# A small network beside a streaming statistics pass: fewer array passes, one transfer queue, deeper buffers

## The chip, the cores and the metric

The kernel runs on one core of one Trainium2 chip. The core has a matrix engine (TensorE, "PE" in the profile, with its weight loads as "PEld"), a vector engine (VectorE, "DVE"), a scalar engine (ScalarE, "ACT"), a general engine (GpSimd, "POOL") and a synchronising engine (SyncE, "SP"). SP and ACT can each put transfers on a queue of their own; the engine that issues a transfer stands still while it waits for its turn ("SPq", "ACTq" in the profile). The metric is the device time of one execution in microseconds (us), as the median of several. All data are fp32.

## The reference, cut to what matters

Two layers are computed one after the other. Each normalizes its input over groups of channels, applies a convolution whose weights differ at every position and batch (they come out of a small network), and adds the result to its input.

```python
S2, B, CI, CO, L, K, A, H = (32, 32, 64, 64, 256, 3, 16, 128)
def _ln(h, g, b):                      # mean and variance over the 128 hidden units
    ...
h  = relu(_ln(z @ W1 + b1, g1, be1))   # z: (B, L, 16); first small network
w  = (h @ W2 + b2).reshape(B, L, CI, CO, K)
hb = relu(_ln(z @ Wb1 + bb1, gb1, beb1))           # second small network
bias = (hb @ Wb2 + bb2).transpose(0, 2, 1)
out = einsum('sbilk,bliok->sbol', windows_of(x), w) + bias[None]
# x = x + conv(groupnorm(x)), for layer 0 and then for layer 1
```

The statistics of the first normalization run over all of the input x, 32 x 32 x 64 x 256 fp32 numbers, so nothing of the convolution of layer 0 can be finished before x has been read once.

## The kernel before

The kernel has two parts. A **first phase** streams x through on-chip memory in 16 transfers of 4 MB, and VectorE takes statistics of it (256 `bn_stats` instructions). Beside that, in the same stretch of time, the small networks of both layers are evaluated for all batches, in 32 steps of two batches each: a step makes the hidden units `hd` and the bias `bd`, which go to HBM and are read back later. The **main part** then runs the convolutions of both layers. The change touches only the first phase.

A step is split over three turns of the pipeline. In turn `s` the kernel projects step `s`, scales step `s-1` and makes the bias of step `s-2`:

```python
class Hidden:
    def __init__(self, stage, zts, small, i):
        self.zt = zts[i % NZ]                       # NZ = 4, one z tile for a step
        ...
        self.sq = flat[:, i % 3 * w : ...]          # 3 buffers
        self.ht = flat[:, (3 + i % 4) * w : ...]    # 4 buffers, both networks
        self.bs = flat[:, 7 * w + i % 4 * L : ...]  # 4 buffers

    def project(self):                              # PE, then ACT
        self.p1 = ps_g.tile([P, NBLK, 2, P], ...)   # NBLK = 4
        for k in range(NBLK):
            for r in range(0, P, C):                # C = 64: two groups of array columns
                a = k * P + r
                nc.tensor.matmul(self.p1[r : r + C, k], self.zt[:, a : a + C], self.t["wc"], ...)
        nc.scalar.activation(self.sq, self.p1..., AF.Square)

    def sums(self):        # POOL: 7 additions that halve the width, to the variance
    def root(self):        # ACT: square root
    def scale(self):
        nc.vector.reciprocal(self.var, self.var)
        nc.vector.tensor_tensor(...)                # first half of the rows
        for k in range(n, 2 * NBLK):
            nc.scalar.activation(hs[:, k], p1[:, k], AF.Copy, scale=...)   # second half
        for k in range(NBLK):
            for net in range(2):
                nc.tensor.transpose(p2[:, net, k * P : (k + 1) * P], hs[:, 2 * k + net, :], ident)
        for net in range(2):
            nc.scalar.activation(self.ht[:, net, :], p2[:, net, :], AF.Relu, ...)
        nc.scalar.dma_start(out=hd[self.i]..., in_=self.ht[:, 0, :]...)
    def bias(self):
        for b in range(2):
            nc.tensor.matmul(p3[b * C : (b + 1) * C], self.t["Wb2"], self.ht[:, 1, ...], ...)
        nc.scalar.activation(self.bs, p3..., AF.Identity, bias=...)
        for b in range(2):
            nc.scalar.dma_start(out=bd[self.i][b]..., in_=self.bs[...]...)
```

The steps are laid between the statistics instructions, three of those to each half turn:

```python
def step(s, half):
    if half == 0:
        if s - 1 in made: made[s - 1].root()
        if s < U // 2:                              # U // 2 = 32
            made[s] = Hidden(stage, zts, small, s)
            made[s].project(); made[s].sums()
            load_z(s + NZ, nc.scalar)
    else:
        if s - 1 in made: made[s - 1].scale()
        if s - 2 in made: made.pop(s - 2).bias()

SQ = SV // NH * GT                                  # 16 statistics for one 4 MB load
first, last = 4, (NQ - 3) * SQ                      # NQ = 16, so last = 208
n = U + 4                                           # 68 half turns
when = {first + k * (last - first) // n: k for k in range(n)}
for i in range(NQ * SQ):                            # 256
    if i in (2, first + n):
        center(stage, small[k], k)                  # take the mean off the small weights
    if i in when:
        step(*divmod(when[i], 2))
    if i == (NQ - 2) * SQ:
        first_weights()                             # first weights of the main part, PE and ACT
    bn_stats(...)
    if i % SQ < SQ - 1: continue
    if q + 3 < NQ: load(q + 3)                      # on SP, into the place just read
    ...                                             # W2 in four parts, hidden units, on SP
```

Three places hold loads of x, so a load goes out when the statistics three loads earlier are done. In the program as it is built, the transfers of both queues take eight completion semaphores in turn, in the order of the program: before a transfer is issued, its engine waits until the transfer eight places earlier has landed, whichever queue that was on.

Of the kernel before, what the change touches and what calls it, by code (L numbers as in the profile page):

```python
# [23 lines left out]
FP = mybir.dt.float32  # L24
AF = mybir.ActivationFunctionType
ALU = mybir.AluOpType
# [4 lines left out]
P = 128  # L31
# [10 lines left out]
def conv_layers(ctx: ExitStack, tc: tile.TileContext, xs: bass.AP, xp: bass.AP, layers: list, out: bass.AP):  # L42


    nc = tc.nc
    B, _, M, S = xp.shape
    SH, C, L = S // 2, P // 2, 2 * M
    A = layers[0]["z"].shape[0]
# [10 lines left out]
    U = NL * B  # L59
    SV = 4  # L60
    BLK = 2 * L
    NBLK = BLK // P
    NZ = 4
    RING = 3
    assert 2 * C == P and NT * S == P and M == P and BLK == 512 and EB == 2 * E

# [50 lines left out]
    def load_b2(n):  # L117
        nc.sync.dma_start(out=b2[n], in_=layers[n]["b2"])
# [20 lines left out]

    def load_small(stage, par, n):  # L140

        t = {}
        for name in ("wc", "vec", "Wb2"):
            shape = list(par[name].shape)
            t[name] = stage.tile(shape, FP, name=f"{name}_{n}")
            nc.sync.dma_start(out=t[name], in_=par[name])
        return t

    def center(stage, t, n):

        wc = t["wc"]
        m = stage.tile([A + 1, 2], FP, name=f"wm_{n}")
        nc.vector.tensor_reduce(m, wc, AX.X, ALU.add)
        nc.vector.tensor_scalar(m, m, -1.0 / P, None, ALU.mult)
        nc.vector.tensor_tensor(wc, wc, m[:, :, None].to_broadcast([A + 1, 2, P]), ALU.add)  # L155

    class Hidden:


        def __init__(self, stage, zts, small, i):  # L160
            self.stage, self.i, self.t = stage, i, small[i // (B // 2)]
            self.zt = zts[i % NZ]

            flat = xn.rearrange("p b m s -> p (b m s)")
            w = 2 * NBLK * P
            self.sq = flat[:, i % 3 * w : (i % 3 + 1) * w].rearrange("p (n h) -> p n h", h=P)
            self.ht = flat[:, (3 + i % 4) * w : (4 + i % 4) * w].rearrange("p (n f) -> p n f", f=BLK)
            self.bs = flat[:, 7 * w + i % 4 * L : 7 * w + (i % 4 + 1) * L]
            self.bs = self.bs.rearrange("p (t a m) -> p t a m", t=NT, a=2)

        def project(self):
            self.p1 = ps_g.tile([P, NBLK, 2, P], FP, tag="pg", name="p1")
            for k in range(NBLK):
                for r in range(0, P, C):
                    a = k * P + r
                    nc.tensor.matmul(  # L176
                        self.p1[r : r + C, k], self.zt[:, a : a + C], self.t["wc"], start=True, stop=True
                    )
            nc.scalar.activation(self.sq, self.p1.rearrange("p k n h -> p (k n) h"), AF.Square)  # L179

        def sums(self):
# [10 lines left out]
        def scale(self):  # L192
            nc.vector.reciprocal(self.var, self.var)  # L193
            hs, p1 = self.sq, self.p1.rearrange("p k n h -> p (k n) h")
            n = NBLK
            nc.vector.tensor_tensor(  # L196
                hs[:, 0:n], p1[:, 0:n], self.var[:, 0:n, None].to_broadcast([P, n, P]), ALU.mult
            )
            for k in range(n, 2 * NBLK):
                nc.scalar.activation(hs[:, k], p1[:, k], AF.Copy, scale=self.var[:, k : k + 1])  # L200
            p2 = ps_g.tile([P, 2, BLK], FP, tag="pg", name="p2")
            for k in range(NBLK):
                for net in range(2):
                    nc.tensor.transpose(p2[:, net, k * P : (k + 1) * P], hs[:, 2 * k + net, :], ident)  # L204
            for net in range(2):
                nc.scalar.activation(  # L206
                    self.ht[:, net, :],
                    p2[:, net, :],
                    AF.Relu,
                    bias=self.t["vec"][:, 2 * net + 1 : 2 * net + 2],  # L210
                    scale=self.t["vec"][:, 2 * net : 2 * net + 1],
                )
            nc.scalar.dma_start(
                out=hd[self.i].rearrange("b p f -> p b f"),
                in_=self.ht[:, 0, :].rearrange("p (b f) -> p b f", b=2),
            )

        def bias(self):
            p3 = ps_c.tile([P, L], FP, tag="pc", name="p3")
            for b in range(2):  # L220
                nc.tensor.matmul(  # L221
                    p3[b * C : (b + 1) * C],
                    self.t["Wb2"],
                    self.ht[:, 1, b * L : (b + 1) * L],
                    start=True,
                    stop=True,
                )
            nc.scalar.activation(
                self.bs,
                p3.rearrange("p (a t m) -> p t a m", a=2, t=NT),  # L230
                AF.Identity,
                bias=self.t["vec"][:, 4:5],
            )
            for b in range(2):
                nc.scalar.dma_start(  # L235
                    out=bd[self.i][b].rearrange("t o l -> o t l"),
                    in_=self.bs[b * C : (b + 1) * C].rearrange("p t a m -> p t (a m)"),
                )
# [3 lines left out]
    def bn_stats(out, y, g):  # L242
        e = E // 2
        nc.vector.bn_stats(out, y.rearrange("p o (a m) -> p o a m", a=2)[:, :, :, g * e : (g + 1) * e])  # L244

    def first_phase(first_weights):


        NQ = NH * B // SV
        w = SV * CH * LT  # L250
# [7 lines left out]
        def load(q, step=SV):  # L258
            for j in range(0, SV, step):
                nc.sync.dma_start(  # L260
                    out=xv[q][:, j : j + step], in_=xs[:, q * SV + j : q * SV + j + step]
                )

        def work(stage):
            zts = []
            for j in range(NZ):
                zts.append(stage.tile([A + 1, BLK], FP, name=f"zt_{j}"))
                nc.gpsimd.memset(zts[j], 1.0)

            def load_z(i, eng):  # L270
                if i < U // 2:
                    n, j = divmod(i, B // 2)
                    eng.dma_start(out=zts[i % NZ][0:A], in_=layers[n]["z"][:, j * BLK : (j + 1) * BLK])

            small = [load_small(stage, layers[0], 0)]
            load_z(0, nc.sync)
            load(0, 1)
            for j in range(1, NZ):
                load_z(j, nc.sync)
            load(1)  # L280
            small.append(load_small(stage, layers[1], 1))
            load(2)
            for n in range(NL):
                load_b2(n)
            made = {}

            def step(s, half):

                if half == 0:
                    if s - 1 in made:  # L290
                        made[s - 1].root()
                    if s < U // 2:
                        made[s] = Hidden(stage, zts, small, s)
                        made[s].project()
                        made[s].sums()
                        load_z(s + NZ, nc.scalar)
                else:
                    if s - 1 in made:
                        made[s - 1].scale()
                    if s - 2 in made:  # L300
                        made.pop(s - 2).bias()

            SQ = SV // NH * GT
            first, last = 4, (NQ - 3) * SQ
            n = U + 4
            when = {first + k * (last - first) // n: k for k in range(n)}
            for i in range(NQ * SQ):
                if i in (2, first + n):
                    k = int(i > 2)
                    center(stage, small[k], k)  # L310
                if i in when:
                    step(*divmod(when[i], 2))
                if i == (NQ - 2) * SQ:
                    first_weights()
                u, g = divmod(i, GT)
                q, j = divmod(u, SV // NH)
                bn_stats(first_parts[:, g, u, 0, :], xu[q][:, j], g)
                if i % SQ < SQ - 1:
                    continue
                if q + 3 < NQ:  # L320
                    load(q + 3)
# [392 lines left out]
```

## Time and profile before

| what | value |
|---|---|
| time, median of 3 runs | 4096.45 us (4092.12 to 4099.84) |
| span of the profiled execution | 4089.9 us |
| PE busy over the span | 3927.3 us (96%) |
| last statistics instruction of the first phase ends | 309.5 us |
| first product of the main part starts | 342.6 us |
| moved from the start to 320 us | 93.10 MB, 291 GB/s on average |

The page divides the span into 40 slices, and one slice is about 102 us. The first phase therefore fills three slices, and its own limits have to be read from windows of the trace, not from the totals. "PEclk" is the clock granted to the matrix engine, as a share of full speed. "Issue" in a chain of waits is time in which an engine waited for nothing that the profile shows, and "ACTq L235" is ScalarE busy with handing a transfer of line 235 to its queue.

### The profile page before, as it was taken

What the parts mean: (1) busy time and instruction counts of PE and PEld (TensorE: products, weight loads), DVE (VectorE), ACT (ScalarE), POOL (GpSimd) and SP (SyncE); (2) the same over time, 40 slices, a digit from 0 to 9 for tenths busy, and PEclk for the clock granted to TensorE, in tenths of its full rate; (3) what the DMA queues carried; (4) which work ended last, traced back from release to release, by engine and by line L of the source; (5) the groups of instructions that cost most, each with busy time, mean ns of one, the idle gap of its engine ahead of it and who ended that gap; (6) DMA issues with size and microseconds to landing.
All of it is one profiled execution on the core that took longest, in us unless ns stands there. A gap on an engine that the chain in (4) does not pass through costs nothing.

```text
span 4089.9 us, 194766 instructions
## 1 busy us (share of the span) xinstructions
PE 3927.3 (96%) x91064; PEld 3737.5 (91%) x91064; DVE 2602.2 (64%) x2934; ACT 1337.8 (33%) x4480; POOL 1946.6 (48%) x638
## 2 busy tenths in 40 slices
PE   6888999999999999999998999999999999999999
PEld 3447999999999999999998999999999999999999
DVE  4566666666666676666666565656555565656565
ACT  4553323233333333232323332323333333323332
POOL 3435435534553454345443655545554455445541
PEclk6558999999999999999999999999999999999999
DMA  8876777777777777777777544444444454445442
GB/s 305 309 284 160 195 174 195 175 191 179 184 187 183 187 182 186 173 194 172 190 171 190 178 150 146 153 143 155 154 145 158 140 166 133 160 139 169 137 148 89
DMA packets 654877, 718.55 MB, mean 176 GB/s; under 512 B 567378, under 2 KB 584052, under 8 KB 585588
## 3 DMA queue, kind: packets, MB, share of 16 engines
q1 hardware_dynamic: 627060, 692.59, 59.9%
q8 instruction: 711, 11.65, 1.2%
q10 hardware_dynamic: 27008, 13.51, 1.1%
q14 instruction: 98, 0.80, 0.1%
HBM read 492.08 MB, written 213.91 MB: 173 GB/s over the span
## 4 chain that ended last, share of the span: by engine, by line
PE 88%; DVE 6%; DMA 2%; issue 2%; ACT 1%; POOL 1%; ACTq 1%; SPq 0%; DVEq 0%; POOLq 0%
PE pg L482 50%; PE pc L528 23%; PE pg L483 12%; DVE wall L494 2%; DVE parts L244 2%; PE p L176 2%; PE p L204 1%; DMA room<-in_xs_dram 1%; DVE room L538 1%; POOL xn L469 1%; ACTq L235 0%; DMA bd<-xn 0%; PE p L221 0%; DMA hd<-xn 0%; ACT xn L179 0%
## 5 line engine op out<-in xcount | busy, mean ns | idle before, releaser
L482 PE MATMUL pg<-hT,w2t 128*64 128x128 f32 x24576 | 2737.1, 273 | 28.2 <-DVE wall L494 11.2
L483 PE MATMUL pg<-hT,w2t 128*64 128x128 f32 x24576 | 2736.5, 273 | 4.3 <-issue 3.9
L482 PEld LDWEIGHTS pg<-hT,w2t 128*64 128x64 f32 x24576 | 2681.5, 137 | 55.9 <-DVE wall L494 23.6
L483 PEld LDWEIGHTS pg<-hT,w2t 128*64 128x64 f32 x24576 | 2682.2, 137 | 7.8 <-issue 6.8
L494 DVE TENSOR_TENSOR wall<-pg,b 64x1024 f32<-64x1024 f32 x1527 | 1855.6, 1220 | 688.9 <-PE pg L483 685.2
L505 ACT ACTIVATE wall<-pg,b 64x128 f32<-64x128 f32 x4168 | 1191.7, 479 | 2585.2 <-DVE wall L494 2157.6
L451 POOL TENSOR_TENSOR xn<-room,gmean 128x2048 f32<-128x2048 f32 x124 | 572.7, 4619 | 1758.1 <-PE pc L528 1728.2
L528 PEld LDWEIGHTS pc<-wall,xn 128*32 128x32 f32 x40960 | 932.2, 111 | 99.4 <-issue 83.9
L528 PE MATMUL pc<-wall,xn 128*32 128x128 f32 (+2 forms) x40960 | 974.2, 253 | 50.8 <-issue 37.8
L538 DVE TENSOR_TENSOR room<-pc,room 128x512 f32<-128x512 f32 x512 | 354.2, 692 | 656.2 <-PE pc L528 583.6
L451 POOL TENSOR_TENSOR xn<-xn,rstd 128x2048 f32<-128x2048 f32 x124 | 656.5, 5294 | 9.7
L418 POOL TENSOR_TENSOR room<-room,bt 128x2048 f32<-128x2048 f32 x128 | 588.5, 4597 | 120.2 <-DMA bt<-bd 49.6
L244 DVE BATCH_NORM_STATS2 parts<-room 128x6 f32<-128x256 f32 (+1 forms) x592 | 241.5, 453 | 8.7
L187 POOL TENSOR_TENSOR xn<-xn 128x512 f32<-128x512 f32 (+2 forms) x192 | 104.1, 542 | 156.3 <-ACT xn L179 143.8
L176 PE MATMUL p<-wc,zt 17*64 17x256 f32 x512 | 116.1, 628 | 12.3 <-DVE wc L155 12.3
L204 PEld LDWEIGHTS p<-ident,xn 128*128 128x128 f32 x256 | 47.4, 207 | 87.9 <-issue 66.1
L176 PEld LDWEIGHTS p<-wc,zt 17*64 17x64 f32 x512 | 53.7, 217 | 71.8 <-issue 71.0
L204 PE MATMUL p<-ident,xn 128*128 128x128 f32 x256 | 69.6, 438 | 50.2 <-DVE xn L196 35.9
L244 DVE BATCH_NORM_STATS2 parts<-wall 128x6 f32<-128x512 f32 x160 | 97.7, 677 | 11.2 <-DMA wall<-in_xs_dram 11.2
L193 DVE RECIPROCAL var<-var 128x8 f32<-128x8 f32 x32 | 6.5, 203 | 111.0 <-ACT var L190 111.0
L206 ACT ACTIVATE xn<-p,vec 128x512 f32<-128x512 f32 x64 | 46.3, 773 | 22.1 <-PE p L204 22.1
L179 ACT ACTIVATE xn<-p 128x1024 f32<-128x1024 f32 x32 | 32.6, 1019 | 36.0 <-PE p L176 35.7
(58 smaller groups left out, 239.5 us busy)
## 6 DMA issues: line engine op xcount, KB each, us to landing
bt<-bd SPq DMA_DIRECT2D x512, 256.0 KB, 6.5
room<-in_xp_dram SPq DMA_DIRECT2D x64, 1024.0 KB, 9.4
room<-in_xs_dram SPq DMA_DIRECT2D x64, 1024.0 KB, 8.6
x<-room SPq DMA_DIRECT2D x64, 1024.0 KB, 5.3
x1p<-room SPq DMA_DIRECT2D x512, 128.0 KB, 6.8
room<-x1p SPq DMA_DIRECT2D x64, 1024.0 KB, 8.0
room<-x SPq DMA_DIRECT2D x64, 1024.0 KB, 8.3
out_dram<-room SPq DMA_DIRECT2D x64, 1024.0 KB, 4.9
```

The source lines that it names most:

```text
L176: nc.tensor.matmul(self.p1[r : r + C, k], self.zt[:, a : a + C], self.t["wc"], start=True, stop=True)
L187: nc.gpsimd.tensor_tensor(to, self.sq[:, :, 0:w], self.sq[:, :, w : 2 * w], ALU.add)
L204: nc.tensor.transpose(p2[:, net, k * P : (k + 1) * P], hs[:, 2 * k + net, :], ident)
L244: nc.vector.bn_stats(out, y.rearrange("p o (a m) -> p o a m", a=2)[:, :, :, g * e : (g + 1) * e])
L418: nc.gpsimd.tensor_tensor(y, y, bts.pop(v), ALU.add)
L451: nc.gpsimd.tensor_tensor(o, i, b.to_broadcast(list(o.shape)), op)
L482: nc.tensor.matmul(pg[0:C, k, :], w[:, k0 * C : (k0 + 1) * C], h0, start=True, stop=True)
L483: nc.tensor.matmul(pg[C:P, k, :], w[:, k1 * C : (k1 + 1) * C], h1, start=True, stop=True)
L494: nc.vector.tensor_tensor(place(rows, a), pg[rows].rearrange("p o (t m) -> p t m o", t=NT), b2[n][rows, kind, None, None, o0 : o0 + OG].to ...
L505: nc.scalar.activation(place(rows, a)[:, :, :, k], pg[rows, k].rearrange("p (t m) -> p t m", t=NT), AF.Identity, bias=b2[n][rows, kind, o0 ...
L528: nc.tensor.matmul(pc[t * S : (t + 1) * S, n0 - q * EB : n1 - q * EB, :], xn[:, u % 2, t * MT + p + 1, :], wall[:, t, a : a + (n1 - n0) * CH],
L538: nc.vector.tensor_tensor(part, pc.rearrange("p (m a) o -> p o a m", a=2), part, ALU.add)
```

## The change

The change rebuilds how the small networks are fed and drained in the first phase. It does five things.

1. **Projections in two groups of array rows.** The contraction has 17 rows (16 inputs and a row of ones for the bias). The z tile and the weights are laid out twice, at partitions 0 and 32, so that half of the blocks go through array rows 0 to 31 and the other half through rows 32 to 63. With the two groups of columns that were there, four products can be in the array at a time.
2. **All transfers by SP's queue.** The stores of hidden units and biases, and the loads of z, move from ScalarE's queue to SP's.
3. **Buffers.** Hidden units that are stored get 6 buffers and those that are only read by the bias product get 2 (4 for both before); biases get 8 (4 before); squares get 2 (3 before). The z tiles hold two steps each, and there are 3 of them.
4. **Weights centred first.** The centring goes ahead of the first statistics instruction (`i == 0` in place of 2), and the steps begin at `i == 1` in place of 4.
5. The end of the steps (`last`) stays, and so does everything after the first phase. The spreading of the statistics, by 4 matmuls in the first layer and by 24 in the second, is the same in both kernels.

```diff
-    NZ = 4
+    NZ = 3
+    ZB = 2
+    R = 32
...
+        t = {"wc": stage.tile([R + A + 1, 2, P], FP, name=f"wc_{n}")}
+        nc.gpsimd.memset(t["wc"], 0.0)
+        for r in (0, R):
+            nc.sync.dma_start(out=t["wc"][r : r + A + 1], in_=par["wc"])
...
-            self.zt = zts[i % NZ]
+            self.zt = zts[i // ZB % NZ][:, i % ZB * 2 * P : (i % ZB + 1) * 2 * P]
...
-            self.sq = flat[:, i % 3 * w : (i % 3 + 1) * w]...
-            self.ht = flat[:, (3 + i % 4) * w : (4 + i % 4) * w]...
-            self.bs = flat[:, 7 * w + i % 4 * L : 7 * w + (i % 4 + 1) * L]
+            self.sq = flat[:, i % 2 * w : (i % 2 + 1) * w]...
+            self.ht = [flat[:, (4 + j) * BLK : (5 + j) * BLK] for j in (i % 6, 6 + i % 2)]
+            self.bs = flat[:, 6 * w + i % 8 * L : 6 * w + (i % 8 + 1) * L]
...
-            for k in range(NBLK):
+            for k in range(NBLK // 2):
                 for r in range(0, P, C):
-                    a = k * P + r
-                    nc.tensor.matmul(
-                        self.p1[r : r + C, k], self.zt[:, a : a + C], self.t["wc"], start=True, stop=True
-                    )
+                    for j in range(2):
+                        rows = slice(j * R, j * R + A + 1)
+                        nc.tensor.matmul(
+                            self.p1[r : r + C, 2 * j + k],
+                            self.zt[rows, k * P + r : k * P + r + C],
+                            self.t["wc"][rows],
+                            start=True,
+                            stop=True,
+                        )
...
-            nc.scalar.dma_start(                     # hd; the two stores of bd likewise
+            nc.sync.dma_start(
...
-            def load_z(i, eng):                      # one transfer for a step
+            def load_z(b):                           # two transfers, on SP, for two steps
...
-                        load_z(s + NZ, nc.scalar)
+                        if s % ZB == ZB - 1:
+                            load_z(s // ZB + NZ)
...
-            first, last = 4, (NQ - 3) * SQ
+            first, last = 1, (NQ - 3) * SQ
...
-                if i in (2, first + n):
+                if i in (0, first + n):
```

More of the change, by code (lines that the diff above doesn't have):

```diff
@@ L140, in load_small @@
     def load_small(stage, par, n):
-        t = {}
-        for name in ("wc", "vec", "Wb2"):
+        t = {"wc": stage.tile([R + A + 1, 2, P], FP, name=f"wc_{n}")}
+        nc.gpsimd.memset(t["wc"], 0.0)
+        for r in (0, R):
+            nc.sync.dma_start(
+                out=t["wc"][r : r + A + 1], in_=par["wc"]
+            )
+        for name in ("vec", "Wb2"):
             shape = list(par[name].shape)
@@ L151, in center @@
         wc = t["wc"]
-        m = stage.tile([A + 1, 2], FP, name=f"wm_{n}")
+        m = stage.tile([R + A + 1, 2], FP, name=f"wm_{n}")
         nc.vector.tensor_reduce(m, wc, AX.X, ALU.add)
         nc.vector.tensor_scalar(m, m, -1.0 / P, None, ALU.mult)
-        nc.vector.tensor_tensor(wc, wc, m[:, :, None].to_broadcast([A + 1, 2, P]), ALU.add)
+        nc.vector.tensor_tensor(wc, wc, m[:, :, None].to_broadcast([R + A + 1, 2, P]), ALU.add)
     class Hidden:
@@ L161, in __init__ @@
             self.stage, self.i, self.t = stage, i, small[i // (B // 2)]
-            self.zt = zts[i % NZ]
+            self.zt = zts[i // ZB % NZ][:, i % ZB * 2 * P : (i % ZB + 1) * 2 * P]
             flat = xn.rearrange("p b m s -> p (b m s)")
             w = 2 * NBLK * P
-            self.sq = flat[:, i % 3 * w : (i % 3 + 1) * w].rearrange("p (n h) -> p n h", h=P)
-            self.ht = flat[:, (3 + i % 4) * w : (4 + i % 4) * w].rearrange("p (n f) -> p n f", f=BLK)
-            self.bs = flat[:, 7 * w + i % 4 * L : 7 * w + (i % 4 + 1) * L]
+            self.sq = flat[:, i % 2 * w : (i % 2 + 1) * w].rearrange("p (n h) -> p n h", h=P)
+            self.ht = [flat[:, (4 + j) * BLK : (5 + j) * BLK] for j in (i % 6, 6 + i % 2)]
+            self.bs = flat[:, 6 * w + i % 8 * L : 6 * w + (i % 8 + 1) * L]
             self.bs = self.bs.rearrange("p (t a m) -> p t a m", t=NT, a=2)
@@ L172, in project @@
             self.p1 = ps_g.tile([P, NBLK, 2, P], FP, tag="pg", name="p1")
-            for k in range(NBLK):
+            for k in range(NBLK // 2):
                 for r in range(0, P, C):
-                    a = k * P + r
-                    nc.tensor.matmul(
-                        self.p1[r : r + C, k], self.zt[:, a : a + C], self.t["wc"], start=True, stop=True
-                    )
+                    for j in range(2):
[6 more added lines that the diff above has]
+                            stop=True,
+                        )
             nc.scalar.activation(self.sq, self.p1.rearrange("p k n h -> p (k n) h"), AF.Square)
@@ L206, in scale @@
                 nc.scalar.activation(
-                    self.ht[:, net, :],
+                    self.ht[net],
                     p2[:, net, :],
@@ L212, in scale @@
                 )
-            nc.scalar.dma_start(
+            nc.sync.dma_start(
                 out=hd[self.i].rearrange("b p f -> p b f"),
-                in_=self.ht[:, 0, :].rearrange("p (b f) -> p b f", b=2),
+                in_=self.ht[0].rearrange("p (b f) -> p b f", b=2),
             )
@@ L223, in bias @@
                     self.t["Wb2"],
-                    self.ht[:, 1, b * L : (b + 1) * L],
+                    self.ht[1][:, b * L : (b + 1) * L],
                     start=True,
@@ L234, in bias @@
             for b in range(2):
-                nc.scalar.dma_start(
+                nc.sync.dma_start(
                     out=bd[self.i][b].rearrange("t o l -> o t l"),
@@ L266, in work @@
             for j in range(NZ):
-                zts.append(stage.tile([A + 1, BLK], FP, name=f"zt_{j}"))
+                zts.append(stage.tile([R + A + 1, ZB * BLK // 2], FP, name=f"zt_{j}"))
                 nc.gpsimd.memset(zts[j], 1.0)
-            def load_z(i, eng):
-                if i < U // 2:
-                    n, j = divmod(i, B // 2)
-                    eng.dma_start(out=zts[i % NZ][0:A], in_=layers[n]["z"][:, j * BLK : (j + 1) * BLK])
+            def load_z(b):
+                if b * ZB < U // 2:
+                    n, i = divmod(b * ZB, B // 2)
+                    z = layers[n]["z"][:, i * BLK : (i + ZB) * BLK].rearrange("a (k j f) -> a k j f", k=ZB, j=2)
+                    for j in range(2):
+                        nc.sync.dma_start(
+                            out=zts[b % NZ][j * R : j * R + A].rearrange("a (k f) -> a k f", k=ZB),
+                            in_=z[:, :, j],
+                        )
             small = [load_small(stage, layers[0], 0)]
-            load_z(0, nc.sync)
+            load_z(0)
             load(0, 1)
             for j in range(1, NZ):
-                load_z(j, nc.sync)
+                load_z(j)
             load(1)
@@ L307, in work @@
             for i in range(NQ * SQ):
-                if i in (2, first + n):
-                    k = int(i > 2)
+                if i in (0, first + n):
+                    k = int(i > 0)
                     center(stage, small[k], k)
```

## The prediction

> **What bounds the kernel now.** I read the page first, then the busy time by stretches, then the chain of waits through the middle of the first phase, then who waited for whom, and last the queues.
>
> ```profile
> PE 3927.3 (96%) x91064; PEld 3737.5 (91%) x91064; DVE 2602.2 (64%) x2934; ACT 1337.8 (33%) x4480; POOL 1946.6 (48%) x638
> ...
> PEclk6558999999999999999999999999999999999999
> ```
>
> ```profile
> core 0: us, PE busy (x) PEld busy (x) DVE busy (x) ACT busy (x) POOL busy (x), PEclk, DMA share, GB/s
> 0.00:21.70 21.70, 7.32 (x32) 3.77 (x32) 9.07 (x19) 4.19 (x5) 5.98 (x17) 1.00 0.90 341
> 21.70:275.70 254.00, 205.97 (x848) 104.68 (x848) 140.09 (x253) 129.22 (x278) 107.18 (x217) 0.53 0.82 295
> 275.70:309.50 33.80, 23.73 (x304) 21.01 (x304) 33.78 (x57) 26.39 (x93) 7.02 (x2) 0.80 0.82 299
> 309.50:340.00 30.50, 19.24 (x252) 14.60 (x255) 18.95 (x34) 10.05 (x31) 5.51 (x3) 0.67 0.25 54
> 340.00:4089.90 3749.90, 3671.05 (x89637) 3593.46 (x89629) 2400.36 (x2574) 1167.95 (x4075) 1820.94 (x399) 1.00 0.61 167
> ```
>
> The page says that the matrix engine is the bound, and for 3749.9 of 4089.9 us it is: 98% busy at full clock. The change touches none of that. What it can touch are the first 309.5 us. There no engine is full: in the long stretch from 21.7 to 275.7 PE is busy 81% at about half clock, DVE 55%, the DMA engines 82%. A stretch like that is bound by a chain, and the chain is this:
>
> ```profile
> 249.28 3.63 PE p L176 x16
> 252.91 0.02 issue
> 252.94 1.02 ACT xn L179
> 253.96 0.27 ACT xn L200
> 254.23 0.04 issue
> 254.27 1.25 PE p L204 x4
> 255.52 1.05 PE p L221 x4
> 256.58 3.63 PE p L176 x16
> ```
>
> That is one turn, 7.30 us from projection to projection (249.28 to 256.58): the projection 3.63, its squares on ACT 1.02, the first scaled copy that ACT could not start before them 0.27, the second half of the transposes 1.25, the bias products 1.05. Nothing of DVE is in it. But the scaling of step 0 is at 21.7 us and that of step 31 at 275.0, so the 31 turns between took 253.3 us, 8.17 each and not 7.30. The missing 0.87 x 31 = 27 us is in the queues:
>
> ```profile
> ACT var L190 <- issue: 48.9, 22, 4.4
> ACT var L190 <- DMA bd<-xn: 12.3, 1, 12.3
> SPq L260 <- DMA hd<-xn: 88.7, 5, 24.4
> SPq L260 <- DVE parts L244: 56.0, 11, 7.2
> ```
>
> ACT stands before its root (L190) for 48.9 us while it issues stores, and 12.3 us at one stroke for a store that had to land. The loads of x (L260) waited 88.7 us for stores of hidden units, because of the eight completion semaphores that go round. DVE's line in the same view, "DVE var L193 <- ACT var L190", says 111.0 us: the statistics wait for the small network, not for their data, for which DVE lost 11.2 us, 9.0 of them at the start.
>
> **What the Trainium skill says.** "TensorEngine Tiling (Array Packing)", Key Properties: different tiles of the array run weight loads and matmuls in parallel; its Gotcha 1 adds that two row tiles must not write the same PSUM bank at once. Here block k of one row group and block k+2 of the other are in different banks (a block is 1 KB of a partition, so two blocks fill a 2 KB bank). The trace before has the column half of this: the 16 instructions of a turn last 628 ns each and together only 3.63 us, so two are in the array at a time. No trace here has row groups yet. "TensorE: Matmul & The Clock Gate", Part 3, measured 3.07 times for four row groups, so I take two row groups at somewhat under 2 times. "DMA: Bandwidth & Descriptors", Issuing engines are not separate DMA queues: issuing from two engines saves only issue time. The trace can't show that yet, but it means that one queue costs no bandwidth by itself, and that what moves is who waits. The same page, Specifications, gives a ceiling of 435 GB/s; the window from 185 to 190 us, with a DMA share of 1.00, moved 421.
>
> **The change part by part.**
>
> *Row groups.* 8 pairs at 3.63 / 8 = 0.45 us become 4 groups of four: 4 x 0.45 = 1.8 us, and I allow 1.9 to 2.0. The projection is on the chain, so a turn falls by about 1.7, from 7.30 to 5.6 us.
>
> *Other loops of a turn.* POOL: square 1.0, then six sums 3.65 and a last one 0.2, root 0.3, with gaps about 5.4 us, since ACT takes the root of one step before the squares of the next. DVE: six statistics at 0.60 (25 in 14.91 us, at 275.6) and 0.92 for reciprocal and scaling, 4.5 us. Both are below 5.6, POOL only just. So compute gives 5.6.
>
> *Queue.* The stores leave ACT: the 48.9 + 12.3 us no longer stand in ACT's order. In SP's order they wait for the same eight semaphores, but behind them stand only the loads of x (three places ahead) and buffers 6 and 8 steps deep (33 us and more at 5.6). I take all of the 27 us that the chain lost as gone, if DMA can follow.
>
> *Start.* Centring no longer waits for two statistics, and the steps begin three statistics earlier: scaling of step 0 then stands behind 10 statistics that begin near 10.5 us, at about 16.5 in place of 21.7. That gives 5 us. Two more small transfers ahead of the first load cost about 0.9 us of issue, in this number.
>
> *End.* From the scaling of step 31 to the last statistics it is 34.5 us now (275.0 to 309.5), 57 statistics; `last` is unmoved, so I keep it.
>
> By compute alone: 16.5 + 31 x 5.6 + 34.5 = 224.6 us in place of 309.5, a gain of 85 us, 2.1%.
>
> *Can DMA follow?* In the view of the queues for 0 to 320 us, SP's queue moved 79.34 MB and ACT's 13.51:
>
> ```profile
> q1 hardware_dynamic: 5396, 79.34, 65.6%
> q10 hardware_dynamic: 27008, 13.51, 14.5%
> ```
>
> 65.6% of 320 is 210 us and 14.5% is 46 us, 256 together, of which about 12 lie after the statistics (0.61 of the last 20 us). So 244 us at the packets' present times. The loads on SP's queue were slowed by the stores beside them: at 421 GB/s its 79.34 MB take 188 us, and less about 12 for what comes later and plus 46 the least is 222 us. By a load: 4.19 MB of x at 421 GB/s is 10.0 us, with 2.67 turns of stores at 46 / 32 = 1.44 us each 3.8, together 13.8, and about 1 us at the point where the queue holds small stores only and waits for receipts: 14.8. Fifteen loads are 222, the four parts of W2 (6.3 MB) 15, start 3, and behind the last store of a bias one more load (10 us) whose 16 statistics take 9.6; overlap of those takes off some 10. That comes to about 250 us. So DMA, not the chain, will set the end: near 250 us, with 225 as the floor by compute and 222 by bytes. The gain I expect is 309.5 - 250 = 60 us, and 4096.5 - 60 = 4036.
>
> **The rivals.**
>
> *One queue stalls itself.* All transfers now stand in one order: a load of x behind a store that isn't computed yet waits for it, and each waits for the one eight places before. A turn has four small transfers on average (one store of hd, two of bd, one of z), so a load comes after about 11 transfers, and eight hold 0.75 of a load or 3 to 4 MB, enough in flight for about 9 us. If SP stands 2 to 3 us for each load, 15 x 2.5 = 37 us come back and the phase ends near 285: 4070. For it speaks the 88.7 us of L260 behind hd; against it, that hd waited there because ACT was late, and that DVE rarely ran dry.
>
> *Row groups don't overlap in fp32.* Then the turn stays at 7.30 and only the queue waits and the start go: 27 + 5 = 32 us, 4064. For it: nothing before has two row groups. Against: columns do overlap in fp32.
>
> *All of the compute gain arrives.* If the DMA engines hold over 400 GB/s with the stores mixed in, the phase ends at 225 to 230 and the time is 4012 to 4017. Against it: from 120 to 220 us, the densest stretch, they moved 322 GB/s at a share of 0.90, which is 358 at full share; the roughly 87 MB of the phase at 358 are 243 us.
>
> *Nothing is gained.* That would need something later to wait. After the phase the order is statistics, spreading, normalization, and each starts when the one before ends; the first weights on ACT (26 us) begin with the 224th statistic and move along. I see nothing for it.
>
> **Range and chances.** Taking 55% for the main line (4025 to 4048), 20% for a self-stalling queue (4045 to 4075), 13% for row groups without overlap (4055 to 4070), 9% for the full gain, and 3% for anything worse, I get 4036 us, with 8 in 10 between 4012 and 4066. Faster by over 2% means under 4014.5, that is a phase of under 228 us, against two floors of 225 and 222: 9%. Slower by over 2%: 2%. Within: 89%.
>
> **What would show it.** In the trace after: the 16 instructions of L176's successor in about 1.9 us, and four overlapping; a turn of 5.6 us in the chain where loads are in time; no ACTq pieces in the chain; ACT's "issue" wait before the root gone; DVE waiting for loads of x in the middle of the phase, far over 11.2 us in sum, with a DMA share of 0.93 or more; the last statistics near 250 us; the stretch from there to the end unchanged near 3780 us. I am wrong if DVE still waits for the root for 100 us with DMA under 0.85 (a chain or the queue's order), if the projection stays above 3 us, or if the main part changes in length.

## The result, and the profile after

| | before | changed |
|---|---|---|
| time, median | 4098.15 us (4 runs) | 4066.91 us (4 runs, 4054.18 to 4068.89) |
| ratio, 95% interval | | 0.992 (0.9897 to 0.9943) |
| scaling of step 0 / of step 31 begins | 21.4 / 274.7 us | 20.4 / 219.8 us |
| one turn, on average | 8.17 us | 6.43 us |
| from the scaling of step 31 to the last statistics | 34.8 us | 51.8 us |
| last statistics of the first phase end | 309.5 us | 271.6 us |

The changed kernel is faster by 31 us, 0.8%. Run once more beside other kernels it took 4067.67 us, 0.9925 (0.9913 to 0.9938). The executions that the profiles show are the fastest of each kernel, 4092.12 and 4054.18 us, and lie 37.9 us apart, as far as the ends of the statistics do. The page after, its lines that answer to those of before:

```profile
PE 3862.2 (95%) x91064; PEld 3711.9 (92%) x91064; DVE 2602.6 (64%) x2934; ACT 1337.0 (33%) x4480; POOL 1946.2 (48%) x639
...
PEclk7569999999999999999999999999999999999999
```

The busy time by stretches, cut within 1 us of the same events as before (scaling of step 0, of step 31, last statistics, first product):

```profile
core 0: us, PE busy (x) PEld busy (x) DVE busy (x) ACT busy (x) POOL busy (x), PEclk, DMA share, GB/s
0.00:20.40 20.40, 3.81 (x32) 2.85 (x32) 7.19 (x15) 4.80 (x5) 9.46 (x25) 1.00 0.73 260
20.40:219.80 199.40, 145.47 (x848) 77.81 (x848) 140.50 (x254) 127.89 (x277) 103.76 (x210) 0.58 0.93 345
219.80:271.60 51.80, 24.35 (x304) 21.19 (x304) 35.59 (x61) 29.43 (x105) 7.01 (x2) 0.70 0.92 352
271.60:303.40 31.80, 18.73 (x296) 14.80 (x296) 21.32 (x38) 6.93 (x19) 5.04 (x3) 0.77 0.33 78
303.40:4052.10 3748.70, 3669.79 (x89584) 3595.20 (x89584) 2398.02 (x2568) 1167.93 (x4075) 1820.92 (x399) 1.00 0.61 166
```

The gain is in the second line, 254 us before and 199 now. The third has given back 17 of it by the events of the table. The DMA share of the second line rose from 0.82 to 0.93. The chain of waits through one undisturbed turn:

```profile
37.40 1.96 PE p L185 x16
39.44 1.02 ACT xn L192
40.47 0.27 ACT xn L213
40.78 1.25 PE p L217 x4
42.03 1.05 PE p L234 x4
43.08 1.98 PE p L185 x16
```

The projection takes 1.96 us in place of 3.63, and the turn from projection to projection is 5.68 us in place of 7.30. The same view at the end of the phase:

```profile
216.50 14.24 DMA wall<-in_xs_dram
230.75 0.57 SPq L248
231.42 14.98 DMA room<-in_xs_dram
246.41 2.90 DMA bd<-xn
249.57 12.29 DMA xn<-in_xs_dram
261.97 9.60 DVE parts L257 x16
```

No computing engine is in it until the last 16 statistics: one load of x lands, SP issues a bias store that waited for it, and only then the next load goes out, twice in a row. The second time the load also waits 2.90 us for that bias store to land, since the last load overwrites the tile (`xn`) that holds the buffers of the small network. The load that left at 231.4 could have left at 212.8 as far as its place is concerned, since VectorE was done with it then. The view of who waited for whom, to 320 us, shows the same for the whole phase:

```profile
DVE var L206 <- ACT var L203: 42.4, 25, 7.6
DVE parts L257 <- DMA wall<-in_xs_dram: 23.8, 7, 6.2
PE p L185 <- DMA zt<-in_L_conv_z_dram: 20.1, 3, 7.3
...
SPq L248 <- DMA wall<-in_xs_dram: 29.5, 7, 7.6
SPq L248 <- DMA room<-in_xs_dram: 18.0, 4, 9.0
SPq L248 <- DMA w2t<-in_L_conv_W_dram: 13.9, 4, 4.1
```

ScalarE's queue waits are gone, and the wait of VectorE for the root fell from 111.0 to 42.4 us. In their place VectorE waits for x (23.8 us here, 36.5 with the two other places that x is loaded to), PE for z (20.1), and SP stands 61.4 us at bias stores (L248) until a load of x or of W2 has landed. One such place in SP's order:

```profile
73.44 0.54 SPq L273 DMA_DIRECT2D room<-in_xs_dram  x1
74.50 0.38 SPq L226 DMA_DIRECT2D hd<-xn  x1
74.98 1.52 SPq L248 DMA_DIRECT2D bd<-xn  x2
76.59 1.06 SPq L289 DMA_DIRECT2D zt<-in_L_conv_z_dram  x2
77.74 0.41 SPq L226 DMA_DIRECT2D hd<-xn  x1
78.24 9.38 SPq L248 DMA_DIRECT2D bd<-xn  x2
87.79 0.49 SPq L273 DMA_DIRECT2D wall<-in_xs_dram  x1
```

The load of 73.44 lands 13.6 us later, at 87.0. The eighth transfer after it is the second bias store of the pair at 78.24; it is issued only then, and the next load stands behind it.

So a new wait stands on SP, and the DMA engines are nearly full. The question for the experiments is which of the two holds the phase at 271.6 us and not at the 250 I had expected.

### The profile page after: what moved, and what is told of

It is laid out like the page before. It is cut to its first block, busy times and chain, and to the rows that moved or that the text cites. A ratio compares the mean times of both kernels' runs of the same rounds, so it can differ in the third digit from the quotient of the medians.

```text
span 4052.1 us, 194865 instructions
## 1 busy us (share of the span) xinstructions
PE 3862.2 (95%) x91064; PEld 3711.9 (92%) x91064; DVE 2602.6 (64%) x2934; ACT 1337.0 (33%) x4480; POOL 1946.2 (48%) x639
## 3 DMA queue, kind: packets, MB, share of 16 engines
q1 hardware_dynamic: 654616, 706.13, 61.4%
## 4 chain that ended last, share of the span: by engine, by line
PE 87%; DVE 5%; DMA 3%; issue 2%; POOL 2%; ACT 1%; SPq 0%; DVEq 0%; POOLq 0%; ACTq 0%
PE pg L502 50%; PE pc L548 23%; PE pg L503 12%; DVE wall L514 2%; DVE parts L257 1%; DMA wall<-in_xs_dram 1%; DMA zt<-in_L_conv_z_dram 1%; DVE room L558 1%; DMA hd<-xn 1%; PE p L185 1%; POOL xn L489 1%; PE p L217 0%; POOL xn L200 0%; POOL xn L471 0%; DMA room<-in_xs_dram 0%
## 5 line engine op out<-in xcount | busy, mean ns | idle before, releaser
L257 DVE BATCH_NORM_STATS2 parts<-wall 128x6 f32<-128x512 f32 x160 | 97.7, 678 | 23.8 <-DMA wall<-in_xs_dram 23.8
L185 PE MATMUL p<-wc,zt 17*64 17x256 f32 x512 | 59.5, 603 | 27.4 <-DMA zt<-in_L_conv_z_dram 20.1
L185 PEld LDWEIGHTS p<-wc,zt 17*64 17x64 f32 x512 | 27.2, 206 | 58.8 <-issue 33.3
L219 ACT ACTIVATE xn<-p,vec 128x512 f32<-128x512 f32 x64 | 46.3, 774 | 21.4 <-PE p L217 21.4
L213 ACT ACTIVATE xn<-p,var 128x128 f32<-128x128 f32 x128 | 36.5, 373 | 10.5 <-DVE xn L209 10.4
```

Of the source, the lines that this page charges most:

```text
L185: nc.tensor.matmul(self.p1[r : r + C, 2 * j + k], self.zt[rows, k * P + r : k * P + r + C], self.t["wc"][rows], start=True, stop=True,)
```

## The experiments

Theory A is the work of the DMA engines: share times length is 0.92 x 271.6 = 250 us in the changed kernel and 0.82 x 309.5 = 254 before. Theory B says that what counts is the stores leaving ScalarE's order. Theory C says that on one queue the eight completion semaphores hold the loads of x up. The main part after the statistics lasted 3780 to 3803 us in the profiled executions, with nothing of it changed between the two kernels (3780.5 and 3794.9 in the two profiles of the changed kernel), so the verdicts rest on the end of the statistics in each profile as well as on the times.

**The row groups alone** (rows_only). The kernel before, with only the projection and the z layout of the change:

```diff
 # abridged: the changed kernel, with these back as before:
-            nc.sync.dma_start(out=hd...); nc.sync.dma_start(out=bd...); z on nc.sync
+            nc.scalar.dma_start(out=hd...); nc.scalar.dma_start(out=bd...); z on nc.scalar
+            # 3 squares, 4 + 4 hidden units, 4 biases; steps from i = 4, centring at i = 2
```

> The kernel before with the row groups (and the z layout they need) alone: stores and z on ScalarE's queue, old buffers, old start. Theory A (the work of the DMA engines now sets the phase: share 0.92 of 271.6 us is 250 us of work, 0.82 of 309.5 was 254 before): the turn falls to about 6.5 us (5.6 and the old queue waits of 0.87), the last statistics end near 275 to 282 us, the DMA share rises to 0.88 or more, the time is 4062 to 4075, most of the gain. Theory B (what counts is that the stores left ScalarE's order): ScalarE waits for its stores longer as the turn gets shorter, the phase ends above 295 us and the time is 4082 or more.

Measured: 4103.05 us, 1.0009 (1.0000 to 1.0017); the statistics end at 308.0, the turn is 8.08 us. Nothing was gained, though 16 instructions now take 2 us. Who waited for whom:

```profile
ACT var L203 <- issue: 44.0, 25, 5.2
ACT var L203 <- DMA hd<-xn: 23.7, 3, 8.1
```

ScalarE waits before the root as long as before (44.0 us of issue, and 23.7 for stores of hidden units): what the array gave back, its queue took. Theory A is out for this kernel, whose DMA share is still 0.82.

**The queue without the row groups** (no_rows). The deeper buffers, z on SP and the early start stay in. Each projection contracts all 49 rows against weights of which the other group's rows are zero:

```diff
-        t = {"wc": stage.tile([R + A + 1, 2, P], ...)}      # both copies under each other
+        t = {"wc": stage.tile([R + A + 1, 2, 2, P], ...)}   # copy j alone in block j, zeros else
-                            self.zt[rows, k * P + r : k * P + r + C], self.t["wc"][rows],
+                            self.zt[:, k * P + r : k * P + r + C], self.t["wc"][:, j],
```

> The changed kernel with one group of array rows (each projection contracts 49 rows, the other half of the weights being zero); queue, buffers, z transfers and start as in the change. Both theories: 16 instructions take about 3.6 us again and the turn is at least 7.3 us. Theory A: 20.4 + 31 x 7.3 + 35 to 45 = 282 to 292 us for the last statistics, 4077 to 4088, DMA share 0.85 to 0.88. Theory B: the queue alone brings most of the change, 4070 or less, so the row groups are worth under 5 us.

Measured: 4086.41 us, 0.9967 (0.9957 to 0.9976); statistics end at 282.8, turn 7.32 us. In the chain of waits a projection starts at 97.56 us and takes 3.68, the next starts at 104.96, and no transfer is waited for in between. Without the row groups the change frees the chain of its waits (8.17 to 7.32 a turn, 26 us) and stops there. It is theory A's number, but the reason is the chain: the DMA share is 0.89.

**The stores back on ScalarE's queue** (act_stores). Everything else as in the change:

```diff
-            nc.sync.dma_start(out=hd[self.i]...)      # and the two of bd
+            nc.scalar.dma_start(out=hd[self.i]...)
```

> The changed kernel with the stores of hidden units and biases back on ScalarE's queue; row groups, buffers, z on SP and start stay. Theory A (DMA work): the same bytes in the same packets, so the last statistics end within 6 us of 271.6 and the time is 4060 to 4073. Theory B (the stores in ScalarE's order are what cost): ScalarE's issue waits come back, 50 us or more in sum, the turn goes to 6.5 us or more, time 4080 or more. Theory C (the order on one queue holds the loads up): loads go out earlier than now and z lands sooner, 4045 to 4058.

Measured: 4109.4 us, 1.0022 (1.0015 to 1.0029), slower than before the change; statistics end at 317.8, turn 8.44 us. Its waits:

```profile
ACT var L203 <- issue: 38.7, 23, 6.0
ACT var L203 <- DMA hd<-xn: 35.4, 6, 9.4
```

Theory B stands for this part: with these waits, 74 us, and 14.8 more at the bias (L241) in ScalarE's order, row groups, buffers and the early start bring nothing. Theory C's version of it (loads go out earlier) did not happen.

**One bias store in place of two** (merged). The bias is laid out so that a step stores it at once:

```diff
-    bd = [dram.tile([2, NT, C, LT], ...)]
+    bd = [dram.tile([NT, 2, C, LT], ...)]
-            for b in range(2):
-                nc.sync.dma_start(out=bd[self.i][b]..., in_=self.bs[b * C : (b + 1) * C]...)
+            nc.sync.dma_start(out=bd[self.i].rearrange("t b o l -> (b o) t l"), in_=self.bs...)
```

> The changed kernel with the two bias stores of a step made into one transfer of twice the size (the bias is laid out with the quarter outermost, packets as long as before), so a turn puts 3 small transfers on the queue in place of 4. Theory A (DMA work): same bytes and packets, the time stays within 5 us of the changed kernel, 4062 to 4072. Theory C (eight completion semaphores on one queue hold the loads up): eight transfers reach further ahead, SP waits less at the bias stores (61 us now behind loads of x and W2), the last statistics end near 258 to 263 us, time 4052 to 4058.

Measured: 4040.10 us, 0.9855 (0.984 to 0.9869); statistics end at 251.2, turn 5.96 us. This is theory C's side, and more than it had promised (4052 to 4058): the bytes and the packets are those of the changed kernel, one transfer fewer a turn is issued, and 27 us are gone.

**Two stores of hidden units in place of one** (split_hd), the opposite:

```diff
-            nc.sync.dma_start(out=hd[self.i].rearrange("b p f -> p b f"), in_=self.ht[0]...)
+            for b in range(2):
+                nc.sync.dma_start(out=hd[self.i][b], in_=self.ht[0][:, b * L : (b + 1) * L])
```

> The changed kernel with the store of hidden units of a step made as two transfers of half the size: a turn puts 5 small transfers on the queue in place of 4, bytes and packets as before. Slot theory (the eight completion semaphores on one queue hold the loads of x up; 3 a turn gave 4040 us, 4 a turn 4067): the other way by about as much, 4085 to 4105, with SP waiting longer behind loads of x and the DMA share under 0.88. Rival (the merged bias store was simply a better transfer, since it spans 128 partitions and not 64): no change, 4062 to 4072.

Measured: 4086.41 us, 0.9963 (0.995 to 0.9976); statistics end at 289.9. With merged, the changed kernel and this one there are 3, 4 and 5 small transfers a turn for the same bytes. The stretch to the last statistics in merged, and then in split_hd (length; busy time of PE, PEld, DVE, ACT and POOL; clock, DMA share, GB/s):

```profile
0.00:251.19 251.19, 174.45 (x1184) 102.30 (x1184) 183.10 (x328) 162.19 (x386) 120.24 (x237) 0.69 0.97 367
```

```profile
0.00:289.93 289.93, 172.56 (x1184) 101.44 (x1184) 183.06 (x329) 162.36 (x386) 120.17 (x237) 0.64 0.86 319
```

| small transfers a turn | kernel | time, us | statistics end, us | DMA share | share x length, us |
|---|---|---|---|---|---|
| 3 | merged | 4040.10 | 251.2 | 0.97 | 244 |
| 4 | changed | 4066.91 | 271.6 | 0.92 | 250 |
| 5 | split_hd | 4086.41 | 289.9 | 0.86 | 249 |

The work of the DMA engines hardly changes; what changes is how much of the time they have any. Each further transfer a turn costs about 20 us. The rival (a better shape of the bias store) doesn't explain split_hd. In it SP stands at the stores of hidden units (L227):

```profile
SPq L227 <- DMA wall<-in_xs_dram: 46.3, 6, 9.2
SPq L227 <- DMA room<-in_xs_dram: 26.1, 3, 10.2
```

With 16.2 us behind W2 that is 88.6 us behind loads, against 61.4 at L248 in the changed kernel.

One more rival has to be answered: a small transfer keeps SP busy for 0.4 to 0.6 us when it waits for nothing, and 32 of them are 13 to 19 us, nearly the 20. But SP is not short of time. By the same views it stood waiting for ScalarE for 78.1 us in merged, 60.1 in the changed kernel and 31.1 in split_hd. The number of semaphores itself was not varied.

**Is the wait for z a cause?** (z_far)

```diff
-    NZ = 3
+    NZ = 4
```

> The changed kernel with 4 z tiles in place of 3, so that z is asked for two steps earlier. The projection waited 20 us for z in the changed kernel, in three places. If these waits are a cause: they go, and the last statistics end 10 to 15 us earlier, 4052 to 4058. If they only show that the queue is late as a whole: the same load of x is waited for a little later, and the time stays within 5 us, 4062 to 4072.

Measured: 4070.40 us, 0.9925 (0.991 to 0.994); statistics end at 272.7. PE no longer waits for z anywhere in the phase, and the end did not move:

```profile
DVE parts L257 <- DMA wall<-in_xs_dram: 31.1, 8, 9.4
```

With 18.0 and 6.0 us for the loads to the two other places, VectorE waits 55.1 us for x in place of 36.5. The wait for z was a sign of a late queue, not a cause, although the chain of the changed kernel runs through it.

**The buffers** (old_buffers): the changed kernel with 3 squares, 4 + 4 hidden units and 4 biases, as before.

```diff
-            self.ht = [flat[:, (4 + j) * BLK : (5 + j) * BLK] for j in (i % 6, 6 + i % 2)]
+            self.ht = [flat[:, (6 + j) * BLK : (7 + j) * BLK] for j in (i % 4 * 2, i % 4 * 2 + 1)]
```

> The changed kernel with the buffers of before (3 squares, 4 hidden units of both networks, 4 biases). Stores land a median of 12 to 14 us after issue, and SP issues them some 10 us after they are ready, 22 to 24 us together, against 4 turns of 6.4 us. If the deeper buffers are needed: ScalarE and PE wait for landing stores, 4075 to 4090. If four are just enough: 4062 to 4072, the same as the changed kernel.

Measured: 4066.02 us, 0.9922 (0.9908 to 0.9935); statistics end at 268.2. The deeper buffers bring nothing by themselves. ScalarE does wait for landing stores, 32.3 us before L219, but VectorE then waits 21.3 us for x in place of 36.5: again one wait for another.

**The row groups on a queue that follows** (merged_no_rows): the edits of merged and no_rows together.

> The merged kernel with one group of array rows, as in no_rows: with the queue out of the way, what are the row groups worth? If the two parts add up only when neither hides the other: the turn goes back to the 7.32 us of no_rows, which merging can't shorten since it is the chain of PE and ScalarE, so 4080 to 4090 as no_rows, and the row groups are worth 40 to 48 us here (19 in the changed kernel, none on ScalarE's queue). If merging also shortened waits in that chain: under 4075.

Measured: 4089.12 us, 0.998 (0.9972 to 0.9988); statistics end at 282.4. By the end of the statistics the row groups bring 1.5 us on ScalarE's queue (309.5 to 308.0), 11 on SP's with two bias stores (282.8 to 271.6), and 31 with one (282.4 to 251.2). Merging without them brings 0.4 us (282.8 to 282.4): with a turn of 7.3 us the queue has time enough. By the medians the row groups bring 49 us here; the part that the phase doesn't show has no cause on record.

**Is the merged kernel at the limit of the DMA engines?** (no_bd) The bias stores of 31 of the 32 steps are left out, and the main part reads the biases of the first two batches for all:

```diff
-            nc.sync.dma_start(out=bd[self.i]...)
+            if self.i == 0: nc.sync.dma_start(out=bd[self.i]...)
-                src = bd[u // 2][t, u % 2, ...]
+                src = bd[0][t, u % 2, ...]
```

> The merged kernel without the bias stores of 31 of the 32 steps (left out: the biases of all batches but the first two; the main part reads those of the first two everywhere, so the output is another). It takes 4 MB in 256-byte packets and one transfer a turn away. DMA-work theory for the merged kernel (DMA share 0.97 over 251 us): the phase ends 10 to 16 us earlier, near 238, where the turn of 5.7 us takes over (20 + 31 x 5.7 + 35 = 232), time 4024 to 4030. If the merged kernel is bound by its turn already: within 5 us of 4040.

Measured: 4027.20 us, 0.982 (0.9803 to 0.9836).

```profile
0.00:233.25 233.25, 170.52 (x1184) 100.24 (x1184) 182.77 (x328) 158.93 (x376) 119.86 (x237) 0.66 0.95 379
```

The statistics end at 233.3 us, close to the 232 of the turn, and VectorE waits for x only at the start and in two more places (9.7 us in all). So the merged kernel was held by its transfers; with a share of 0.95, the DMA engines are nearly full in this one too. This run takes a transfer a turn away as well as bytes, so it doesn't divide the 18 us between the two.

**The second half of W2 after x** (w2_late), on the merged kernel:

```diff
-                if q + 8 in range(NQ - 4, NQ):
+                if q in (NQ - 12, NQ - 11, NQ - 3, NQ - 2):     # two parts early, two after x
```

> The merged kernel with the second half of W2 (3 MB, not needed before the second half of the first output) loaded after the last load of x, in the stretch where the DMA engines are at a share of about 0.3. DMA-work theory: the phase loses 3 MB at about 370 GB/s, 8 us: 4030 to 4034. Turn theory: within 4 us of 4040. If the stretch after it needs the DMA engines after all: slower than 4044.

Measured: 4038.95 us, 0.9848 (0.9831 to 0.9864). The statistics end at 243.0 us, 8.2 earlier, as the work of 3 MB would have it; the time, which the DMA-work theory put at 4030 to 4034, is 1 us lower than merged, inside the intervals of the two. The gain is shown for the phase and not for the time.

**All together** (best): merged, w2_late, z for four steps at a time, and the first quarter of the first load ahead of the small weights.

```diff
-    NZ = 3; ZB = 2
+    NZ = 2; ZB = 4
+            load(0, 1, 0, 1)                                    # first 1 MB of x before anything
             small = [load_small(stage, layers[0], 0)]
```

> One bias store a step, the second half of W2 after the last load of x, z in batches of four steps (2.5 small transfers a turn on average), and the first quarter of the first load of x ahead of the small weights. The phase of w2_late ended at 243 us; the start gives 3, fewer slots 3 to 5, the turn of 5.7 us sets 20 + 31 x 5.7 + 35 = 232 as the least: 235 to 238, time 4025 to 4033.

Measured: 4034.53 us, 0.9847 (0.9833 to 0.986). The statistics end at 240.3 us; both are just past what was expected. It beats the kernel before by 1.5% and the changed one by 0.8%, and over merged it is not clear of the intervals. Its DMA share to the last statistics is 0.99, so a next step would be to move fewer bytes, or longer packets; no run here tries it. The changed kernel once more, beside it:

> The changed kernel once more, beside the others of this call: 4062 to 4072; its statistics end near 272 us.

Measured: 4067.67 us, statistics end at 272.6.

## Why the prediction was right or wrong

The side and the kind were right: faster, by under 2%, and the first phase is where it was gained. The gain was 31 us where I had 60, and 4066.9 lies at the upper end of the range (4066). The main line (4025 to 4048, the work of the DMA engines sets the end) did not come; the rival's 4070 did. Two signs that I had named for the main line came all the same, 36.5 us of waits for x and a share of 0.93 in the long stretch, so they could not tell the two apart. Merged and split_hd could.

- **Row groups**: right. 16 instructions, 603 ns each on average, in 1.96 to 1.98 us, and an undisturbed turn of 5.68 us (5.6 predicted). The inference "two are in the array at a time" does not follow from the numbers beside it: 16 x 628 ns / 3.63 us is 2.8, and 4.9 by the same sum now, with ends that the profile models. The ratio of the stretches is firm: 3.63 / 1.97 = 1.84 times. No_rows, with the same order of products and 3.68 us, shows that it comes of the row groups. The rival without overlap is out.
- **Queue**: the 27 us of ScalarE's waits were right. No_rows, with the stores off ScalarE's queue and no row groups, gives back 26 us, and act_stores shows that without this part the rest brings nothing. No run moves the stores and leaves the buffers and the start as they were.
- **Start**: mis-sized, 5 us promised and 1.0 measured. The first statistics begin at 13.4 us and not at 10.5: the load of x stands behind six small transfers, and SP waits until 2.9 us for POOL to zero the weights' tile before it issues the first.
- **End**: wrong, 51.8 us and not 34.5, of which 16.0 are waits for the last three loads of x. I had kept the old number since `last` was unmoved, though the loads behind it had moved.
- **DMA**: 250 us is the work of the engines in this kernel (0.92 x 271.6), but not its end. Two steps of the sum to 250 failed. The first is "about 1 us at the point where the queue holds small stores only". From the fifth load on, loads of x left 14.4 to 18.2 us apart where no W2 was about, and 18.2 to 22.6 where it was, not 14.8 and 18.6. About 11 small transfers lie between two loads, and the eighth after a load waits until it has landed, so the next load can't leave earlier; SP stood 61.4 us there, and the share stayed at 0.92. The stores hold their semaphores longer, too: a bias store landed 7.3 us after its issue before (median) and 12.5 us now, on one queue with the loads. From the first load's issue to the last one's it took 244.1 us, where I had 222 + 15 = 237, and 223.6 in merged.
- **The overlap at the end** is the second: it "takes off some 10", and there is none. The last load left at 249.6, landed 12.3 us later, and its statistics took the 9.6 after that, so 22 us in place of 9.6. It is 22 us in merged and split_hd as well. With the first load leaving at 5.4 and not at 3, the three terms (7.1, 12.4 and 2.4 us) make up the 22 us between 250 and 271.6. That merged ends at 251.2 is therefore luck for the sum: its loads leave faster than I had, and its end is longer.
- **The rival "one queue stalls itself"** is what happened, by its second half: each transfer waits for the one eight places before. I gave it 20% because VectorE "rarely ran dry" before. It rarely ran dry because the turn was 8.17 us: the wait that I took as evidence against was hidden by the one that the change removed.
- **"The least is 222 us"**, from loads at 421 GB/s once the second queue is gone: wrong. The engines' work is 244 to 254 us in every kernel here with all the stores and all of W2 in the phase, on two queues (before, 254) or on one (250). That is what "DMA: Bandwidth & Descriptors", Issuing engines are not separate DMA queues, says: the queues share the engines. I had quoted it and still let the loads speed up.
- **Buffers**: I counted on their depth. It was not needed at 4 transfers a turn.
- **Main part**: 3780.5 us after the statistics against 3780.4 in the first two profiles, as said. But the changed kernel's second profile has 3794.9 with the same program, so equality is not shown to better than some 14 us. The medians give 31 us where the phase gives 37.9, and the difference of 7 us stays open.

## What to carry to other kernels

Where transfers take completion semaphores in turn, as here, the places in that round are a resource of their own: count the small transfers between two large ones, and merge them before looking for bandwidth. A chain and a queue that hide each other are priced together. Here the same row groups were worth 1.5, 11 or 31 us of the phase. The stores' move was worth 46 us with the row groups (317.8 to 271.6), and with the buffers and the start 27 without them (309.5 to 282.8). When a wait goes, read every small wait of before as if the large one had not covered it.

## What the runs showed of the hardware that was not expected

The bias stores, 31 of them of 128 KB in packets of 256 bytes, cost about 22 us of the DMA engines' time (0.97 x 251.2 in merged less 0.95 x 233.3 in no_bd, give or take 2.4 us for shares that are rounded to a hundredth). If all of it is their own, 4.06 MB / 22 us = 185 GB/s, against 421 in a stretch with a share of 1.00 before. The times of the 256-byte packets in the traces, added up, give a little less: 18.7 us of the 16 engines in merged and 0.9 in no_bd, so 17.8 us or 228 GB/s; the other packets got shorter by the rest. "DMA: Bandwidth & Descriptors", Specifications, asks for 512 bytes or more for the full rate; both figures agree with that.

The granted clock in the records does not tell the speed of these matmuls. In no_rows it reads 1.00 from 100 to 240 us and the 16 instructions take 3.68 us; before it reads 0.50 there, and they take 3.63.
